# A four-layer graph network on one core: the chain of group bounds run from both ends, the whole-sum rows dealt anew, group matrices six ahead

## The chip, the cores and the metric

The kernel runs on one core of one Trainium2 chip. The metric is the device time of one execution in microseconds (us); less is better. Five engines work side by side, each in the order of its own queue: TensorE (PE in the profile), VectorE (DVE), ScalarE (ACT), GpSimd (POOL) and SyncE (SP), which issues most DMAs. An engine that comes to an instruction whose input isn't there waits, and what is queued behind waits too.

## What is computed

`x` is 2708 nodes x 128 features, `adj` a 2708 x 2708 matrix of weights at or above zero. Four layers follow each other, each `x = layernorm(x + layer(x, adj))`:

- layer 0: `D^-1/2 (adj + I) D^-1/2 x W^T + b`, with D the row sums;
- layer 1, the attention: `XW = x W`, `den[i, j] = exp(leaky_relu(s_row[i] + s_col[j]))`, `num = adj @ den`, `att = den / num`, result `adj @ (att @ XW)`;
- layer 2: a hyperbolic layer around `adj @ xt`;
- layer 3: `adj @ edge + (adj > 0) @ node + (adj < 0) @ node'` and biases.

Only the start of layer 1 is touched by the change. `exp(leaky_relu(a + b))` is the larger of `exp(a + b)` and `exp(0.01 (a + b))`, and which one it is depends on the sign of `a + b` alone. The kernel sorts the rows by one score and the columns by the other, cuts both into at most 26 matching groups of at most 126 nodes, and computes `num` for all columns group by group. For one group it needs the sum over all rows of adj weighted by exp(score), which it carries from group to group, and the group's own rows of adj.

## The kernel before

Nodes are held in NT = 22 tiles of 128 (I call one tile of rows k0 to k21) and NB = 6 column blocks of 512, the last of 148 (c0 to c5). adj is streamed from HBM in tiles `(d, c)`: block row d (4 row tiles), block column c, 1 MB each, or 0.3 MB for c5.

**After layer 0** (lines 1122 to 1162) the scores are ready. Five things then run in one stretch, from 176 to 226 us of the profile:

1. *The whole sum* (`whole_sum`, line 796, called through `sum_rows(n)`, line 1061): n row tiles are multiplied by e1 = exp(score). A row tile takes nine f32 matmuls with one output row each (line 803), dealt by `sums_of` (line 791) to the four column strips at output rows 0, 32, 64 and 96. Strips work side by side. Each strip has one block of 512 columns. Block c4 is cut by q4 = 160 into pieces of 160, 160, 160 and 32, and the last strip takes c5 (148) behind its 32. The row tiles go in the order k0-3, k16-19, k20-21, k4-7, k8-11, k12-15.
2. *The fetches* (`fetch_next`, line 764): adj doesn't fit, so block rows 0 to 3 are fetched again, in order, into 12 places of pool `keep`. A place is free once the whole sum has used up a block row (line 812). From there follow three lots. After k3: (1,2) to (1,5), (2,0), (2,1). After k19: (2,2) to (2,5), (3,0), (3,1). After k7: (3,2) to (3,5), which is 3.45 MB and the last.
3. *The group bounds* (lines 1189 to 1247). 384 sampled scores cut the sorted order. Lines 1203 to 1217 count, for each sample, how many samples lie more than CAP = 126 nodes below it (`prev`). Three PE transposes spread prev along the free axis (`prev_ps`), line 1234 copies it to `prev_row`, and a chain of GM = 26 dependent DVE steps follows: `v[g+1]` = the number of entries of prev_row below `v[g]` (line 1239). All 128 partitions do the same.
4. *The lists* (lines 1258 to 1362). From the bounds, DVE makes one-hot grids (c3, then `oh`, lines 1271 and 1277), PE makes running counts (`low`, lines 1288 and 1298), DVE turns them into slots, and for each side i = 0, 1 there are 22 pairs of a DVE one-hot tile (`ohs`, line 1326, ten buffers) and a PE matmul (`list`, line 1328). List 0 gives the row numbers for the gathers (`row_i`), list 1 the column factors `gj_l`.
5. *Spreading a score over the partitions* (lines 1226 to 1232): for each block b, PE transposes (`rb`) and an ACT Exp into `q_b`.

Who comes first on an engine is fixed by hand with `queued(engine...)` (line 190): each instruction traced inside is issued on its engine after the one that the last such block left. It is an order of issue, on engines that work in order. What isn't in such a block is placed by the framework's scheduler. The PE order before is: below, two row tiles, prev_ps, three row tiles, rb0, three, rb1, one, rb2, one, rb3, one, rb4, one, rb5, low, two row tiles, list 0 with one row tile after 8 and after 16 of its matmuls, two row tiles, list 1.

**The attention loop** (`grouped_attention`, line 1402) runs over q = 0 to 51, 26 groups for each half of the columns. Each q has an indirect gather of 128 rows of adj into `rows_g` (line 1415, three ahead), three chunks of `num` (PE 1464), a copy of two carried rows into the next group's rows_g (DVE 1467), Ln (ACT 1469), Exp of its negative (1479), a product (DVE 1483), and `uacc` (PE 1491). The first group's carried rows are copied by nine ACT copies from the whole sum (line 1371) and one DVE copy (1446). `group_matrix(dst, g)` (line 704) makes the weights of num for a group: one PE transpose (707) and one ACT Relu (708). Groups 0 to 2 are made ahead of the loop; in step q group q + 3 follows. rows_g is in pool `cb_b`, opened after `keep` is closed, on the same memory.

The rest (lines 1551 to 1887, layers 2 and 3) streams adj three times more and isn't touched.

Of the kernel before, what the change touches and what calls it, by code (L numbers as in the profile page):

```python
# [30 lines left out]
CAP = 126  # L31
FIRST = NS // P
GM = 26
SENTINEL = 1.0e29
EMPTY = -1.0e5
RC_MAX = 10.0
# [21 lines left out]
def kernel(  # L58
# [51 lines left out]
    def iota(name, n, base, step, channel, dt=F32):  # L110
        nc.gpsimd.iota(iota_i[:, :n], pattern=[[step, n]], base=base, channel_multiplier=channel)
        t = const.tile([P, n], dt, tag=name, name=name)
        nc.gpsimd.tensor_copy(t, iota_i[:, :n])
        return t

    iota_b = iota("iota_b", P, 0, 1, 0, BF16)
    part_f = iota("part_f", 1, 0, 1, 1)
    node_z = iota("node_z", NT, -N, P, 1)
    unit0 = iota("unit0", 2, 0, -1, 1)
# [577 lines left out]
    xw_i = col.tile([P, GM], I32, tag="xw_i", name="xw_i")  # L697

    flag_i = col.tile([1, 1], I32, tag="flag_i", name="flag_i")
    v = col.tile([P, GM + 1], F32, tag="v", name="v")  # L700
    sc = col.tile([P, GM], F32, tag="sc", name="sc")
    bi = col.tile([P, GM], F32, tag="bi", name="bi")

    def group_matrix(dst, g):

        pg = ps_tile(f"gb{g}")
        nc.tensor.transpose(pg[:, :P], gj_l[:, g : g + 1].to_broadcast([P, P]), ident)
        nc.scalar.activation(dst[:, g, 2:], pg[:, 2:P], AF.Relu, scale=sc[:, g : g + 1], bias=bi[:, g : g + 1])
# [75 lines left out]

    e1 = c_tile("e1")
    e2 = c_tile("e2")
    q4 = 160
    order = [0, NB - 2, NB - 1, *range(1, NB - 2)]
    steps = iter([(d, i) for d in order for i in range(len(tiles(d)))])

# [50 lines left out]
    with tc.tile_pool(name="tri", bufs=1) as tp:  # L841
# [219 lines left out]
        def sum_rows(n):  # L1061
            with queued(PE):
                return whole_sum(n)
# [104 lines left out]
    with ctx_keep:  # L1168
# [11 lines left out]
        with tc.tile_pool(name="sort", bufs=1) as st_p:  # L1180

            def srt(shape, name, dt=F32, bufs=1, tag=None):
                return st_p.tile(shape, dt, tag=tag or name, name=name, bufs=bufs)
# [7 lines left out]
            for i in range(2):  # L1191
                if i:
                    nc.tensor.matmul(below_s[i][:, :NS], lhsT=ones_b, rhs=counts[:, i, :], start=True, stop=True)
                for q in range(len(SAMPLES)):
# [5 lines left out]
                        stop=True,  # L1200
                    )

            for i in range(2):
                nc.vector.tensor_scalar(
                    lim[:, i, :], below_s[i][:, NS : NS + len(SAMPLES)], float(-CAP), None, op0=ALU.add
                )
                for q in range(len(SAMPLES)):
                    junk = srt([P, NS], f"jp{i}_{q}", F16, 2, "jk")
                    nc.vector.tensor_scalar(
                        junk,  # L1210
                        below_s[i][:, :NS],
                        lim[:, i, q : q + 1],
                        None,
                        op0=ALU.is_lt,
                        op1=ALU.add,
                        accum_out=prev[:, i, q : q + 1],
                    )
            nc.vector.tensor_tensor(prev[:, 0, :], prev[:, 0, :], prev[:, 1, :], op=ALU.max)
            prev_ps = ps_tile("prev_ps")
            sum_rows(2)  # L1220
            with queued(PE):
                for q in range(len(SAMPLES)):
                    nc.tensor.transpose(
                        prev_ps[:, q * P : (q + 1) * P], prev[:, 0, q : q + 1].to_broadcast([P, P]), ident
                    )
            for b in range(NB):
                w, cs = width(b), bslice(b)
                sum_rows(3 if b < 2 else 1)
                with queued(PE):
                    pr = bcast_block(rcl[:, 0, :], b, f"rb{b}")  # L1230
                with queued(ACT):
                    nc.scalar.activation(q_b[:, cs], pr[:, :w], AF.Exp, scale=0.99)
            prev_row = srt([P, NS], "prev_row", F16)
            nc.vector.tensor_copy(prev_row, prev_ps[:, :NS])

            nc.vector.memset(v[:, 0:1], 1.0)
            for g in range(GM):
                junk = srt([P, NS], f"jk{g}", F16, 2, "jk")
                nc.vector.tensor_scalar(
                    junk,  # L1240
                    prev_row,
                    v[:, g : g + 1],
                    None,
                    op0=ALU.is_lt,
                    op1=ALU.add,
                    accum_out=v[:, g + 1 : g + 2],
                )
# [9 lines left out]

            upto = srt([P, 2, NT], "upto")
            nc.vector.tensor_sub(upto, counted[:, :, :NT], counted[:, :, 1:])
            vs = srt([P, GM + 1], "vs")  # L1260
            nc.vector.tensor_scalar(vs, v, float(-NS), None, op0=ALU.add)
            c3 = [srt([P, NT, GM + 1], f"c3_{i}", BF16) for i in range(2)]
            val = [srt([P, NT, 6, GM], f"val{i}", BF16) for i in range(2)]
            oh = [val[i][:, :, 5, :] for i in range(2)]
# [18 lines left out]
            for i in range(2):  # L1283
                for h, (ta, tb) in enumerate(((0, t_a), (t_a, NT))):
                    low[i, h] = acc_tile(2 + 2 * i + h, f"low{i}_{ta}")
                    nn = (tb - ta) * GM
                    with queued(PE):
                        nc.tensor.matmul(
                            low[i, h][:, :nn],
                            lhsT=upper,  # L1290
                            rhs=oh[i][:, ta:tb, :],
                            start=True,
                            stop=False,
                            skip_group_check=True,
                        )
                        for t in range(tb - 1):
                            first = max(t + 1, ta)
                            nc.tensor.matmul(
                                low[i, h][:, (first - ta) * GM : nn],
                                lhsT=ones_b,  # L1300
                                rhs=oh[i][:, t, :].unsqueeze(1).to_broadcast([P, tb - first, GM]),
                                start=False,
                                stop=(t == tb - 2),
                                skip_group_check=True,
                            )

            lists = []
            for i in range(2):
# [9 lines left out]
                nc.vector.tensor_reduce(slot[:, i, :], pos[i], AX.X, ALU.add)  # L1318
                nc.vector.tensor_scalar(slot[:, i, :], slot[:, i, :], 2.0, None, op0=ALU.add)
                ps = ps_tile(f"list{i}")  # L1320
                sum_rows(2)
                for t in range(NT):
                    if i == 0 and t in (8, 16):
                        sum_rows(1)
                    ohs = srt([P, P], f"ohs{i}_{t}", BF16, 10, "ohs")
                    nc.vector.tensor_scalar(ohs, iota_b, slot[:, i, t : t + 1], None, op0=ALU.is_equal)
                    with queued(PE):
                        nc.tensor.matmul(
                            ps[:, : 6 * GM],
                            lhsT=ohs,  # L1330
                            rhs=val[i][:, t, :, :].rearrange("p n g -> p (n g)"),
                            start=(t == 0),
                            stop=(t == NT - 1),
                        )
# [53 lines left out]
    def added_up():  # L1388
        below0, okb = (c_tile(n, 1) for n in ("below0", "okb"))
        nc.vector.tensor_reduce(below0, neg_sum, AX.X, ALU.add)  # L1390
        nc.vector.tensor_scalar(below0, below0, 0.0, None, op0=ALU.is_le)
        nc.vector.tensor_scalar(okb, v[:, GM : GM + 1], float(NS), None, op0=ALU.is_equal)
        nc.vector.tensor_mul(okb, okb, below0)
        nc.vector.tensor_scalar(good, good, okb, None, op0=ALU.mult)
        nc.vector.tensor_reduce(gs, good, AX.X, ALU.add)
# [6 lines left out]
    def grouped_attention(u_sb, rows_g):  # L1402
        adj_h = adjT.rearrange("k (h w) -> (k h) w", h=2)
        chunks = [(0, BW), (BW, 2 * BW), (2 * BW, HALF)]
        with tc.tile_pool(name="main", bufs=1) as mp:
# [79 lines left out]
            def aggregate(q):  # L1485
# [12 lines left out]
                if g == GM - 1:  # L1498
                    for c, (ca, cb) in enumerate(chunks):
# [4 lines left out]
                        else:  # L1504
                            with queued(DVE):
                                nc.vector.tensor_copy(dst, src)

            for q in range(3):
                behind = gather(q)
            for g in range(3):  # L1510
# [7 lines left out]
            for q in range(2 * GM + 2):  # L1518
                if q + 3 < 2 * GM:
                    behind = gather(q + 3)  # L1520
                    if q == 3:
                        marks["begun"] = behind
                    if q + 3 < GM:
                        with queued(PE, ACT):
                            group_matrix(w_all, q + 3)
                        group_xw(q + 3, behind)
                t = q - GM - 3
                if 0 <= t < HALF // P:
                    with queued(PE, ACT):
# [444 lines left out]
```

## Time and profile before

| what | us |
|---|---|
| median of three runs (899.6, 901.1, 905.04) | 901.1 |
| the profiled execution's own time | 904.86 |
| its span, first to last instruction | 903.1 |
| PE / DVE / ACT / POOL busy in the span | 846.5 / 555.2 / 388.6 / 206.1 |
| first step of the chain of 26 begins / grid op after it begins | 184.32 / 201.61 |
| last row tile of the whole sum ends | 219.80 |
| first num matmul of the attention loop begins | 226.57 |

In a timeline a line gives the start, the time, the engine, the line of the kernel, the operation, output<-input, the shape and the number of instructions merged, and in square brackets how long the engine stood idle before it and what ended that. In the chain of waits a line gives the start, the time and the work that everything after it waited for. In the windows the columns are the busy time of PE, weight loads, DVE, ACT and POOL, then the granted share of PE's full clock (PEclk), the busy share of the DMA engines, and GB/s. An f32 matmul shows as two instructions, so a row tile has 18.

### The profile page before, as it was taken

The numbers are of one execution on the slowest core, as the hardware profiler recorded it, in microseconds if no ns is written. First come the engines' busy times: TensorE is split into PE (matmuls) and PEld (weight loads), VectorE is DVE, ScalarE is ACT, GpSimd is POOL, SyncE is SP. The second block draws the span as 40 slices with busy tenths as digits, with TensorE's granted clock in tenths as the row PEclk, the third lists the DMA queues.
The fourth block names the chain that finished last, engine by engine and source line by source line (L and its number), as shares of the span: only waits on it lengthen the run. The fifth ranks groups of instructions, "written<-read, shape, count | busy, mean of one in ns | idle before, by whom it ended". The sixth has DMA issues, their size and how long they took to land.

```text
span 903.1 us, 9464 instructions
## 1 busy us (share of the span) xinstructions
PE 846.5 (94%) x3268; PEld 430.0 (48%) x3268; DVE 555.2 (61%) x1189; ACT 388.6 (43%) x681; POOL 206.1 (23%) x176
## 2 busy tenths in 40 slices
PE   3699999698899999999999999989999899999996
PEld 3254454335344445444454444534444555555555
DVE  4777548988788888889971226375644564233313
ACT  3776433215787777777761115273332221000000
POOL 5221000101888885776500000000000000000000
PEclk9799999889899999999999999999999999999997
DMA  9995684596596555445534776496764565463410
GB/s 341 366 356 209 120 248 141 180 383 217 185 380 202 161 150 160 141 154 154 154 121 167 267 269 229 133 336 239 264 224 131 208 215 198 144 253 142 162 39 19
DMA packets 95979, 184.30 MB, mean 204 GB/s; under 512 B 6446, under 2 KB 23551, under 8 KB 95668
## 3 DMA queue, kind: packets, MB, share of 16 engines
q1 hardware_dynamic: 85700, 143.82, 46.2%
q0 software_dynamic: 8352, 37.76, 13.0%
q10 hardware_dynamic: 1872, 2.04, 0.7%
q8 instruction: 28, 0.46, 0.2%
q14 instruction: 27, 0.22, 0.1%
HBM read 179.33 MB, written 4.28 MB: 203 GB/s over the span
## 4 chain that ended last, share of the span: by engine, by line
PE 84%; DMA 9%; DVE 4%; ACT 2%; issue 0%; SPq 0%; DVEq 0%; ACTq 0%
PE a L1584 22%; PE num L1464 13%; PE uacc L1491 13%; PE a L1863 12%; PE a L866 9%; PE a L1872 6%; DMA A<-in_adjT_dram 4%; DMA B<-in_adjT_dram 3%; PE t L803 1%; DMA cb<-in_adjT_dram 1%; PE pp L1821 1%; DVE counts L1051 1%; PE mx L1691 1%; DMA rows_g<-in_adjT_dram,row_i 1%; PE su L251 0%
## 5 line engine op out<-in xcount | busy, mean ns | idle before, releaser
L1415 POOL DMA_INDIRECT rows_g<-in_adjT_dram,row_i x52 | 130.8, 2515 | 90.2 <-PE num L1464 41.2
L1469 ACT ACTIVATE ln<-num,inval,occ_l 128x512 f32<-128x512 f32 x156 | 107.4, 724 | 53.4 <-DVE rows_g L1467 49.4
L1863 PE MATMUL a<-cb,ut 128*128 128x512 f32 (+2 forms) x264 | 125.8, 559 | 1.1 <-DMA cb<-in_adjT_dram 1.1
L1491 PE MATMUL uacc<-att,xw_g 128*128 128x512 f32 (+1 forms) x312 | 126.3, 542 | 0.0
L1872 PE MATMUL a<-mask,node 128*128 128x512 f32 (+2 forms) x264 | 120.3, 537 | 0.7 <-DVE mask L1851 0.7
L1464 PE MATMUL num<-rows_g,w_all 128*128 128x512 f32 (+1 forms) x276 | 113.8, 545 | 0.8 <-ACT ln L1469 0.8
L1584 PE MATMUL a<-cb,q_b 128*128 128x512 f32 (+2 forms) x264 | 111.6, 561 | 1.8 <-DMA cb<-in_adjT_dram 1.8
L866 PE MATMUL a<-A,q_b 128*128 128x512 f32 (+2 forms) x264 | 105.9, 549 | 1.6 <-DMA A<-in_adjT_dram 1.6
L1584 PE MATMUL a<-cb,xw 128*128 128x512 f32 (+2 forms) x264 | 107.3, 550 | 0.0
L1467 DVE COPY rows_g<-num 2x512 f32<-2x512 f32 x150 | 88.0, 612 | 15.4 <-PE num L1464 14.1
L1491 PEld LDWEIGHTS uacc<-att,xw_g 128*128 128x128 f32 x312 | 59.1, 190 | 59.0 <-issue 50.0
L1483 DVE TENSOR_TENSOR att<-att,ln 128x1354 f32<-128x1354 f32 x52 | 80.5, 1548 | 2.0 <-ACT ln L1479 2.0
L1464 PEld LDWEIGHTS num<-rows_g,w_all 128*128 128x128 f32 x276 | 49.5, 190 | 54.0 <-issue 38.9
L1872 PEld LDWEIGHTS a<-mask,node 128*128 128x128 f32 (+1 forms) x264 | 48.5, 193 | 49.4 <-issue 47.6
L230 ACT ACTIVATE sq_l<-s 128x512 f32<-128x512 f32 (+1 forms) x11 | 6.6, 604 | 148.2 <-DVE s L1881 116.7
L1479 ACT ACTIVATE ln<-ln 128x1354 f32<-128x1354 f32 x52 | 69.3, 1333 | 1.7
L1851 DVE TENSOR_SCALAR mask<-cb 128x3072 fp32r<-128x3072 f32 (+5 forms) x24 | 33.5, 1395 | 59.1 <-PE a L1872 58.6
L866 PEld LDWEIGHTS a<-A,q_b 128*128 128x128 f32 (+1 forms) x264 | 45.8, 190 | 49.8 <-issue 46.4
L1584 PEld LDWEIGHTS a<-cb,q_b 128*128 128x128 f32 (+1 forms) x264 | 45.1, 192 | 46.9 <-issue 42.8
L1584 PEld LDWEIGHTS a<-cb,xw 128*128 128x128 f32 (+1 forms) x264 | 45.1, 190 | 46.5 <-issue 46.5
L1074 ACT ACTIVATE xw<-A 128x2048 f32<-128x2048 f32 (+3 forms) x36 | 57.0, 1582 | 7.9 <-DMA b_s<-in_b_dram 4.3
L1456 DVE TENSOR_SCALAR att<-q_b,gj_l 128x1354 f32<-128x1354 f32 x52 | 48.2, 927 | 12.7 <-PE uacc L1491 12.6
(445 smaller groups left out, 900.6 us busy)
## 6 DMA issues: line engine op xcount, KB each, us to landing
cb<-in_adjT_dram SPq DMA_DIRECT2D x15, 2816.0 KB
cb<-in_adjT_dram SPq DMA_DIRECT2D x15, 2560.0 KB
A<-in_adjT_dram SPq DMA_DIRECT2D x25, 1024.0 KB
B<-in_adjT_dram SPq DMA_DIRECT2D x18, 1024.0 KB
cb<-in_adjT_dram SPq DMA_DIRECT2D x3, 814.0 KB
cb<-in_adjT_dram SPq DMA_DIRECT2D x3, 740.0 KB
ut<-in_adjT_dram SPq DMA_DIRECT2D x2, 1024.0 KB
A<-in_adjT_dram SPq DMA_DIRECT2D x5, 296.0 KB
```

The lines of the kernel that those rows point to most:

```text
L866: nc.tensor.matmul(acc[c][:, :w], lhsT=z[:kw, k, :], rhs=t[:kw, i, :w], start=c not in begun, stop=(d == NB - 1 and k == NT - 1), skip_gro ...
L1074: checks[d, c] = nc.scalar.activation(below[:, :nt, :w], t[:, :nt, :w], AF.Relu, scale=-1.0, accum_out=neg_sum[:, NB * c + d : NB * c + d ...
L1415: got = nc.gpsimd.indirect_dma_start(out=gat[q], out_offset=None, in_=adj_h, in_offset=bass.IndirectOffsetOnAxis(ap=row_i[:, h, g : g + 1] ...
L1464: nc.tensor.matmul(num[:, : cb - ca], lhsT=w, rhs=gat[q][:, ca:cb], start=True, stop=True)
L1467: nc.vector.tensor_copy(gat[q + 1][0:2, ca:cb], num[0:2, : cb - ca])
L1469: nc.scalar.activation(ln_n[q][:, ca:cb], num[:, : cb - ca], AF.Ln, scale=occ_l[:, g : g + 1], bias=inval[:, g : g + 1],)
L1479: nc.scalar.activation(ln_n[q], ln_n[q], AF.Exp, scale=-1.0)
L1483: nc.vector.tensor_mul(att[q], att[q], ln_n[q])
L1491: nc.tensor.matmul(uacc[h][c][:, : cb - ca], lhsT=xw_g[:, g, :], rhs=att[q][:, ca:cb], start=(g == 0), stop=(g == GM - 1),)
L1584: nc.tensor.matmul(acc[:, :w], lhsT=weights[:kw, k, :], rhs=pc[:kw, t, :w], start=(k == 0), stop=(k == NT - 1),)
L1863: nc.tensor.matmul(acc[:, :w], lhsT=edge[:ke, k, :], rhs=pc[:ke, t, :w], start=(k == 0), stop=False, skip_group_check=True,)
L1872: nc.tensor.matmul(acc[:, :w], lhsT=node[:kw, k, j, :], rhs=mask[:kw, t - ma, :w], start=False, stop=(k == NT - 1 and j == 1), skip_group_ ...
```

## The change

- **Bounds from both ends.** `far[i, q]`, the 0/1 rows that were thrown away, are kept in BF16 (three buffers) and six ones-matmuls add them up over the partitions: `next_ps` says for each sample how many lie too far beyond it. Partitions 0 to 63 of prev_row hold prev as before, partitions 64 to 127 hold next: an ACT copy of one next_ps to SBUF and a DVE maximum with the other. The chain has GH = 13 steps, one half of the partitions going up, the other down. Two small matmuls with the constant `ends` take row 0 and row 64 of v to all partitions (`both`), and two DVE operations put the 27 bounds together. A third, `reach`, replaces the test of the last bound (line 1392).
- **Whole-sum rows.** q4 becomes 165, so that every strip has 512 + 165 columns. The PE order becomes: below, then one row tile after the first and after the second far matmul, the other far matmuls, prev_ps, three row tiles, rb0, two, rb1, both, one row tile, rb2, rb3, low, rb4, rb5, two, list 0 with one after 8 and after 16, four, list 1 with one after 8 and after 16. The order of the row tiles and the rule of the fetches stay.
- **Buffers.** ohs has four buffers instead of ten.
- **Group matrices.** Groups 3 to 5 are made ahead of the first gather, and step q makes group q + 6.

```diff
@@ the bounds @@
+            far, next_ps = {}, [acc_tile(2, "next0"), acc_tile(5, "next1")]
             for i in range(2):
...
                 for q in range(len(SAMPLES)):
-                    junk = srt([P, NS], f"jp{i}_{q}", F16, 2, "jk")
+                    far[i, q] = srt([P, NS], f"jp{i}_{q}", BF16, 3, "jp")
                     nc.vector.tensor_scalar(
...
+                    with queued(PE):
+                        nc.tensor.matmul(
+                            next_ps[i][:, :NS],
+                            lhsT=ones_b,
+                            rhs=far[i, q],
+                            start=(q == 0),
+                            stop=(q == len(SAMPLES) - 1),
+                        )
+                    if i == 0 and q < 2:
+                        sum_rows(1)
...
-            sum_rows(2)
...
-            for b in range(NB):
+            def spread_rows(b):
                 w, cs = width(b), bslice(b)
-                sum_rows(3 if b < 2 else 1)
                 with queued(PE):
                     pr = bcast_block(rcl[:, 0, :], b, f"rb{b}")
                 with queued(ACT):
                     nc.scalar.activation(q_b[:, cs], pr[:, :w], AF.Exp, scale=0.99)
+            for b in range(2):
+                sum_rows(3 - b)
+                spread_rows(b)
             prev_row = srt([P, NS], "prev_row", F16)
-            nc.vector.tensor_copy(prev_row, prev_ps[:, :NS])
+            next_row = srt([P, NS], "next_row", F16)
+            with queued(ACT):
+                nc.scalar.copy(next_row[64:, :], next_ps[0][64:, :NS])
+            with queued(DVE):
+                nc.vector.tensor_tensor(prev_row[64:, :], next_row[64:, :], next_ps[1][64:, :NS], op=ALU.max)
+            with queued(DVE):
+                nc.vector.tensor_copy(prev_row[:64, :], prev_ps[:64, :NS])
             nc.vector.memset(v[:, 0:1], 1.0)
-            for g in range(GM):
+            for g in range(GH):
...
+            both = ps_tile("both")
+            for i in range(2):
+                with queued(PE):
+                    nc.tensor.matmul(
+                        both[:, i * (GH + 1) : (i + 1) * (GH + 1)],
+                        lhsT=ends[:, i : i + 1].to_broadcast([P, P]),
+                        rhs=v,
+                        start=True,
+                        stop=True,
+                    )
+            sum_rows(1)
+            for b in range(2, NB - 2):
+                spread_rows(b)
             vs = srt([P, GM + 1], "vs")
-            nc.vector.tensor_scalar(vs, v, float(-NS), None, op0=ALU.add)
+            with queued(DVE):
+                nc.vector.tensor_scalar(vs[:, : GH + 1], both[:, : GH + 1], float(-NS), None, op0=ALU.add)
+            with queued(DVE):
+                nc.vector.tensor_scalar(
+                    vs[:, GH + 1 :],
+                    both[:, 2 * GH : GH : -1],
+                    1.0,
+                    vs[:, GH : GH + 1],
+                    op0=ALU.add,
+                    op1=ALU.max,
+                )
...
+            for b in range(NB - 2, NB):
+                spread_rows(b)
+            nc.vector.tensor_tensor(reach, vs[:, GH : GH + 1], both[:, 2 * GH + 1 : 2 * GH + 2], op=ALU.subtract)
@@ the lists @@
-                sum_rows(2)
+                sum_rows(4 if i else 2)
                 for t in range(NT):
-                    if i == 0 and t in (8, 16):
+                    if t in (8, 16):
                         sum_rows(1)
-                    ohs = srt([P, P], f"ohs{i}_{t}", BF16, 10, "ohs")
+                    ohs = srt([P, P], f"ohs{i}_{t}", BF16, 4, "ohs")
@@ the attention loop @@
+            with queued(PE, ACT):
+                for g in range(FIRST, FIRST + 3):
+                    group_matrix(w_all, g)
             for q in range(3):
                 behind = gather(q)
...
                     if q + 3 < GM:
+                        group_xw(q + 3, behind)
+                    if q + FIRST + 3 < GM:
                         with queued(PE, ACT):
-                            group_matrix(w_all, q + 3)
-                        group_xw(q + 3, behind)
+                            group_matrix(w_all, q + FIRST + 3)
```

More of the change, by code (lines that the diff above doesn't have):

```diff
@@ L33 @@
 GM = 26
+GH = GM // 2
 SENTINEL = 1.0e29
@@ L116 @@
     iota_b = iota("iota_b", P, 0, 1, 0, BF16)
+    ends = const.tile([P, 2], F32, tag="ends", name="ends")
+    nc.gpsimd.memset(ends, 0.0)
+    nc.gpsimd.memset(ends[0:1, 0:1], 1.0)
+    nc.gpsimd.memset(ends[64:65, 1:2], -1.0)
     part_f = iota("part_f", 1, 0, 1, 1)
@@ L699 @@
     flag_i = col.tile([1, 1], I32, tag="flag_i", name="flag_i")
-    v = col.tile([P, GM + 1], F32, tag="v", name="v")
+    v = col.tile([P, GH + 1], F32, tag="v", name="v")
+    reach = col.tile([P, 1], F32, tag="reach", name="reach")
     sc = col.tile([P, GM], F32, tag="sc", name="sc")
@@ L786 @@
     e2 = c_tile("e2")
-    q4 = 160
+    q4 = (N - 4 * BW) // 4
     order = [0, NB - 2, NB - 1, *range(1, NB - 2)]
@@ L1207 @@
                 for q in range(len(SAMPLES)):
-                    junk = srt([P, NS], f"jp{i}_{q}", F16, 2, "jk")
+                    far[i, q] = srt([P, NS], f"jp{i}_{q}", BF16, 3, "jp")
                     nc.vector.tensor_scalar(
-                        junk,
+                        far[i, q],
                         below_s[i][:, :NS],
@@ L1232 @@
                     nc.scalar.activation(q_b[:, cs], pr[:, :w], AF.Exp, scale=0.99)
+            for b in range(2):
+                sum_rows(3 - b)
+                spread_rows(b)
             prev_row = srt([P, NS], "prev_row", F16)
-            nc.vector.tensor_copy(prev_row, prev_ps[:, :NS])
+            next_row = srt([P, NS], "next_row", F16)
[5 more added lines that the diff above has]
+                nc.vector.tensor_copy(prev_row[:64, :], prev_ps[:64, :NS])
             nc.vector.memset(v[:, 0:1], 1.0)
-            for g in range(GM):
-                junk = srt([P, NS], f"jk{g}", F16, 2, "jk")
+            for g in range(GH):
+                junk = srt([P, NS], f"jk{g}", F16, 1, "jk")
                 nc.vector.tensor_scalar(
@@ L1391, in added_up @@
         nc.vector.tensor_scalar(below0, below0, 0.0, None, op0=ALU.is_le)
-        nc.vector.tensor_scalar(okb, v[:, GM : GM + 1], float(NS), None, op0=ALU.is_equal)
+        nc.vector.tensor_scalar(okb, reach, 1.0, None, op0=ALU.is_ge)
         nc.vector.tensor_mul(okb, okb, below0)
```

## Prediction

> **What bounds the kernel now.** I read the page first: PE is 84% of the chain that ended last, DMA 9%, and the span's second fifth is where DMA enters. The change lies there, so I read the chain of waits for 186 to 246 us, then the timelines of DVE, ACT and SP, and the windows.
>
> The timeline of DVE shows the chain of 26:
>
> ```profile
> 183.73 0.56 DVE L1234 CAST prev_row<-prev_ps 128x384 f16<-128x384 f32 x1 [1.48 <-PE prev_ps L1223]
> 184.32 0.61 DVE L1239 TENSOR_SCALAR_CACHE_REDUCE jk<-prev_row,v 128x384 f16<-128x384 f16 x1
> ...
> 200.74 0.61 DVE L1239 TENSOR_SCALAR_CACHE_REDUCE jk<-prev_row,v 128x384 f16<-128x384 f16 x1
> ...
> 201.61 0.78 DVE L1271 TENSOR_TENSOR c<-vs,upto 128x594 bf16<-128x594 f32 x1
> ```
>
> A step takes (200.74 - 184.32) / 25 = 0.657 us, 26 take 17.1. But in the chain of waits not one of them appears:
>
> ```profile
> 187.65 12.43 DMA B<-in_adjT_dram
> ...
> 202.19 12.26 DMA B<-in_adjT_dram
> 214.44 0.04 issue
> 214.49 0.41 PE t L803 x2
> 214.90 0.66 PE list L1328 x8
> 215.56 1.28 PE t L803 x15
> 216.83 0.52 PE list L1328 x6
> 217.35 2.45 PE t L803 x30
> 219.80 0.30 PE list L1328 x3
> 220.10 5.41 DMA rows_g<-in_adjT_dram,row_i
> 225.51 0.03 issue
> ...
> 225.61 0.92 DVE rows_g L1446
> ...
> 226.57 3.79 PE num L1464 x4
> ```
>
> The path is the fetches, then row tiles of the whole sum (L803), then the first gather. DVE has row_i at 218.7, yet the gather starts at 220.10, when the last row tile is done: rows_g lies on keep's memory, which the whole sum reads. So num starts 6.77 us after the last row tile, whatever the lists do. The last lot of fetches is issued when row tile k7 ends; the SP queue shows it:
>
> ```profile
> 195.50 1.18 SPq L824 DMA_DIRECT2D B<-in_adjT_dram  x1
> ```
>
> It queues behind transfers that run without a gap (about 386 GB/s from 184 to 210), so its last tile lands at 214.45. And ACT makes q_b only as PE gets to the transposes:
>
> ```profile
> 187.93 0.60 ACT L1232 ACTIVATE q_b<-rb 128x512 f32<-128x512 f32 x1 [12.28 <-PE rb L238]
> 192.23 0.60 ACT L1232 ACTIVATE q_b<-rb 128x512 f32<-128x512 f32 x1 [3.71 <-PE rb L238]
> ```
>
> The windows show PE's clock at half after idle stretches (here 197.5 to 200):
>
> ```profile
> 200.00:202.00 2.00, 1.88 (x10) 0.91 (x14) 1.86 (x8) 0.14 (x1) 0.00 (x0) 0.50 1.05 386
> 202.00:204.00 2.00, 2.00 (x20) 0.56 (x13) 1.97 (x4) 0.46 (x1) 0.00 (x0) 0.69 1.06 389
> ```
>
> [...] 0.50 at 176 to 182, 200 to 202, 224 to 230. [...] In the trace ACT stands 12.28 us in front of the first Exp; nothing overtakes. [...] here x_d is issued at 169.20 and bytes move from 170.0, 0.8 us, which I use.
>
> **The change, part by part.**
>
> *Where the chain starts.* The ACT copy of next_row is queued(ACT) behind the Exp of rb0 and of rb1. Those wait for PE: rb1 stands behind five row tiles. So the chain no longer waits for prev_ps alone but for all of that. PE: far matmuls and the first two row tiles at half clock, as now (4.42 us for two), plus six far matmuls (0.2 to 0.3 each) and a wait for the third far buffer, end with prev_ps at 185.1 (now 183.7). Three row tiles 3.6 (now 183.62 to 187.24) give 188.7, rb0 0.6, two row tiles 2.45, and rb1 starts at 191.7. Exp starts 0.7 later (as 191.54 to 192.23), takes 0.6: 192.95. The copy, by the nearest ACT rows (256 columns 0.38, 512 columns 0.60), 0.5: 193.4. DVE maximum and cast of 384 columns, 0.56 each as L1234: chain start 194.5, against 184.3. **+10.2.**
>
> *The chain.* 13 x 0.657 = 8.5 instead of 17.1: **-8.55.** It ends at 203.05 instead of 201.35.
>
> *Both and vs.* Two f32 matmuls with 14 columns on a cold PE, unpriced in the trace: between 0.3 (a warm transpose) and 0.9; I take 0.6. One more DVE operation, 0.1 to 0.2. Grids start at 204.1 instead of 201.6: **+2.5** in all.
>
> *Up to low.* PE has stood idle since 192.3, over 10 us, so it is at half clock. Behind `both` stand a row tile (2.2 cold, half of 4.42), rb2 and rb3 (0.6 each, rb3 perhaps one Exp later for its buffer): low starts at 207.5, now 204.0. It takes 5.9 as now, and ends at 213.4 instead of 209.9. [...]
>
> *The last lot of fetches.* Now k7 ends before low. In the new order k6 and k7 come after low, rb4 and rb5: 213.4 + 0.85 + 2 x 1.24 = 216.7, against 195.5. The transfers before it have run dry by about 205.5 (214.45 less 3.45 MB at 386 GB/s, 8.9 us). So its bytes lie bare: 216.7 + 0.8 + 8.9 + 0.8 for the end (bytes thin out by 213.7, landing 214.45) = 227.2, against 214.45.
>
> *What PE has after low.* Ten row tiles instead of six, and both lists in front of the end. k6, k7, list 0 with k8, k9, then k10 and k11 end at 224.2; k12 needs the fetch. From its landing: rest of k12 0.4, k13 to k15 3.6, 16 list matmuls. Four ohs buffers let PE run only four ahead of DVE (0.17 each), so 8 take about 0.97 instead of 0.66. Sum 5.95, and I add 0.6 for a clock that may drop again while PE waits (0 to 1.8). The last row tile ends at 233.8, now 219.80: **+14.0.** Were the fetch in time, PE alone would end it at 231.0, +11.2.
>
> *The gather and the start of the loop.* 6.77 as now. Beside it run list 1's end, gj_l, the nine ACT copies (3.6) and now seven group matrices instead of four, three more of 0.44 on ACT: 3.6 + 0.35 + 7 x 0.42 = 6.9 on ACT, about equal to the gather's cover. **+0.2** (0 to 1.4).
>
> *Group matrices.* Their place in a step is unchanged, so the wait of num for the ACT Relu (2.12 us at 234) stays. Steps 20 to 22 lose theirs; a step takes about 4.71 with one (4.66, each fifth 4.93) and 4.55 without: 3 x 0.16, **-0.5.** *q4:* 677 columns instead of 692, 2% of a row tile, already in the sums. reach, ends and the other test: a few 0.1 us operations on DVE and POOL, both with idle time near them; uncovered they would cost under 0.5.
>
> Sum: 14.0 + 0.2 - 0.5 = **+13.7**. On the profile's own 904.86 (span 903.1, 1.8 around it) that is 918.6; the profiled run lies 3.8 above the median of the runs, so on the median **914.8**. About 1% is what a measurement of this kernel can tell from no change.
>
> **Rivals.**
>
> 1. *The copy isn't held* (chance 0.13): it gets in front of the Exps, because ACT is idle from 175.6 to 187.9. For: its input is ready at 184. Against: the queued block. Then the chain runs 185.9 to 194.4, grids at 195.5, low ends at 203.6, the fetch is issued at 206.9, lands at 217.4, and the last row tile ends at 223.4: +3.6 + 0.2 - 0.5, **904.4**. Even so no gain.
> 2. *The saving reaches the path* (0.05): grids at 195.5 instead of 201.6, -6.1, with -0.5 from the group matrices: **894.5**. It decides if k7 ends before 205.5, when the transfers run dry, and the last row tile before 213.7. For: DVE is over 90% busy in that stretch. Against: the chain of waits has no L1239, and after low stand ten row tiles.
> 3. *The queue holds but the fetch is hidden* (0.2, part of the likeliest): PE alone, +11.2 + 0.2 - 0.5, **912**.
>
> **How the numbers follow.** The copy held with the fetch bare has 0.60, with the fetch hidden 0.20; together 910.5 to 919.5, from the clock (-0.6 to +3.2), both (±0.3) and the loop's start (up to 1.2). Rival 1 has 0.13, rival 2 0.05, 0.02 is left for more. Slower by over 1% (above 910.1): 0.74. Within 1%: rival 1, most of rival 2 and the low end of the likeliest, 0.22. Faster: 0.04. The range reaches down to rival 1: 904 to 919.5.
>
> **What would show it.** Right: ACT's next_row copy right behind the second q_b Exp near 193; 13 steps from about 194; PE idle between rb1 and both; a hole in the DMA share from about 206 to 217; the last row tile near 234. Wrong: next_row before q_b; the last lot issued before 206; a gather that starts ahead of the last row tile.

## The result and the profile after

The kernel after takes 916.76 us (median of four runs, 914.91 to 921.35), the kernel before 903.07 us (four runs, 899.6 to 905.37). The ratio is 1.0151, with a 95% interval of 1.0123 to 1.0178: the change makes the kernel slower by about 1.5%. The prediction's 914.8 was reckoned from a median of 901.1 for the kernel before.

The profiled execution after took 921.35 us (span 919.6). It is the highest of the four, 4.6 above their median, so its places are read here against the profiled execution of before (904.86), a difference of 16.5 us. The table gives each place from the start of the first `below` matmul, which is at 177.73 us before and at 178.33 after.

| us from the first `below` | before | after | later by | predicted |
|---|---|---|---|---|
| chain begins | 6.59 | 18.04 | 11.45 | 10.2 |
| grids begin | 23.88 | 28.20 | 4.32 | 2.5 |
| low ends | 32.23 | 38.24 | 6.01 | 3.5 |
| last row tile ends | 42.07 | 59.03 | 16.96 | 14.0 |
| num begins | 48.84 | 65.82 | 16.98 | 14.2 |

From the first num to the last uacc it is 247.38 before and 248.19 after (+0.8), from there to the end 429.15 and 427.26 (-1.9). With the 0.6 by which the stretch begins later, 16.98 + 0.6 + 0.8 - 1.9 = 16.5, the whole difference. That last part of the kernel isn't touched; in the profiles of all kernels here it lies between 424.9 and 429.2, so it varies by 4 us of itself.

The timeline of ACT after answers the two q_b lines of before. The copy stands right behind the second Exp, as its queue has it, and the third Exp waits until 209:

```profile
190.95 0.60 ACT L1248 ACTIVATE q_b<-rb 128x512 f32<-128x512 f32 x1 [14.70 <-PE rb L244]
194.07 0.60 ACT L1248 ACTIVATE q_b<-rb 128x512 f32<-128x512 f32 x1 [2.52 <-PE rb L244]
194.69 0.47 ACT L1258 CAST next_row<-next 64x384 f16<-64x384 f32 x1
209.47 0.60 ACT L1248 ACTIVATE q_b<-rb 128x512 f32<-128x512 f32 x1 [14.30 <-PE rb L244]
```

By the page, DVE's share of the chain of waits has gone from 4% to 7%. The chain of waits after has the steps of the chain of bounds (L1266) in it, which it lacked before. From there it goes through `both`, low, two row tiles (k6 and k7) and the bare fetch to the end of the lists:

```profile
193.45 0.59 PE rb L244 x4
...
196.37 0.63 DVE jk L1266 x2
...
205.01 1.00 PE both L1291 x4
...
217.28 2.43 PE t L810 x30
...
220.41 11.08 DMA B<-in_adjT_dram
...
237.70 5.45 DMA rows_g<-in_adjT_dram,row_i
```

The SP queue issues the first tile of the last lot as k7 ends, 23.9 us later than before (195.50):

```profile
219.39 0.37 SPq L831 DMA_DIRECT2D B<-in_adjT_dram  x1
```

The windows after (PE, weight loads, DVE, ACT, POOL, PEclk, DMA share, GB/s) show what lies on both sides of it:

```profile
196.00:205.00 9.00, 0.00 (x0) 0.02 (x1) 8.40 (x27) 0.00 (x0) 0.00 (x0) 0.59 1.06 378
...
211.00:213.00 2.00, 2.00 (x25) 1.45 (x24) 1.25 (x3) 2.00 (x15) 0.00 (x0) 0.95 0.00 0
...
206.00:220.00 14.00, 14.00 (x155) 8.51 (x154) 10.97 (x26) 8.18 (x50) 0.00 (x0) 0.81 0.02 5
```

While the chain runs, PE does nothing. After it, PE works at half clock until about 211.2 (0.50 from 205 to 211, 0.95 as the mean of 211 to 213). For 14 us the DMA engines carry 5 GB/s; in the ten us after that, the last lot, 316.

What PE waited for in this stretch stands in its own timeline, in the square brackets:

```profile
205.01 1.00 PE L1291 MATMUL both<-v,ends 128*128 128x14 f32 x4 [10.98 <-DVE jk L1266]
...
231.53 0.79 PE L810 MATMUL t<-B,e 128*1 128x165 f32 x20 [1.71 <-DMA B<-in_adjT_dram]
```

So PE stood 10.98 us for the chain, but only 1.71 for the fetch: most of the hole in the transfers lies under PE's own late work. One window each, from the first `below` to the last row tile, first before, then after:

```profile
177.73:219.80 42.07, 39.66 (x462) 18.12 (x463) 37.86 (x136) 10.18 (x55) 1.80 (x1) 0.90 0.88 322
178.33:237.37 59.04, 44.50 (x488) 20.95 (x489) 32.89 (x123) 10.37 (x56) 1.81 (x1) 0.84 0.64 227
```

Of the 17 us that the last row tile came later, PE was idle for 12.1 (14.54 instead of 2.41) and busy for 4.8 more.

### The profile page after: what moved, and what is told of

Its sections match the earlier page's. It is cut to its first block, busy times and chain, and to the rows that moved or that the text cites. A ratio compares the mean times of both kernels' runs of the same rounds, so it can differ in the third digit from the quotient of the medians.

```text
span 919.6 us, 9493 instructions
## 1 busy us (share of the span) xinstructions
PE 849.2 (92%) x3278; PEld 429.4 (47%) x3278; DVE 548.1 (60%) x1166; ACT 389.3 (42%) x682; POOL 206.3 (22%) x179
## 3 DMA queue, kind: packets, MB, share of 16 engines
q0 software_dynamic: 8352, 37.76, 12.8%
## 4 chain that ended last, share of the span: by engine, by line
PE 84%; DVE 7%; DMA 6%; ACT 2%; issue 1%; DVEq 0%; ACTq 0%
PE a L1643 22%; PE num L1519 13%; PE uacc L1546 13%; PE a L1922 11%; PE a L873 9%; PE a L1931 6%; DMA A<-in_adjT_dram 4%; PE t L810 2%; DMA B<-in_adjT_dram 1%; PE pp L1880 1%; DVE counts L1058 1%; DVE jk L1266 1%; PE mx L1750 1%; PE su L257 1%; PE low L1349 1%; DMA rows_g<-in_adjT_dram,row_i 1%
## 5 line engine op out<-in xcount | busy, mean ns | idle before, releaser
L1470 POOL DMA_INDIRECT rows_g<-in_adjT_dram,row_i x52 | 133.7, 2571 | 106.6 <-PE list L1383 57.6
```

What stands on the lines that cost most here:

```text
L1470: got = nc.gpsimd.indirect_dma_start(out=gat[q], out_offset=None, in_=adj_h, in_offset=bass.IndirectOffsetOnAxis(ap=row_i[:, h, g : g + 1] ...
```

## The experiments

The theory after the result: two things in the new queue orders cost the time. The ACT copy stands behind two Exps and holds the chain (the hold), and the row tiles k6 and k7, which free the memory for the last lot, stand behind low (the rows). The rivals: it is the slower lists with four ohs buffers, the group matrices, or a shorter chain that pays as soon as it is let go. Unless said otherwise, "before" is the kernel before in runs on the same chip. All these kernels compute the whole result.

### The hold taken away

In the kernel after, the copy is put on ACT's queue ahead of the first Exp:

```diff
+            next_row = srt([P, NS], "next_row", F16)
+            with queued(ACT):
+                nc.scalar.copy(next_row[64:, :], next_ps[0][64:, :NS])
             for b in range(2):
                 sum_rows(3 - b)
...
-            next_row = srt([P, NS], "next_row", F16)
-            with queued(ACT):
-                nc.scalar.copy(next_row[64:, :], next_ps[0][64:, :NS])
```

> The changed kernel with one move: the ACT copy of next_row is traced ahead of rb0 and rb1, so that it is queued in front of both Exps. Theory (the copy is held behind the Exps): it runs near 185.5 on the changed kernel's clock, the 13 steps begin near 187.6 instead of 196.4, the grids near 197.6 instead of 206.5, the last lot of fetches goes out near 210 instead of 219.4, lands near 222, and the last row tile ends near 228 instead of 237.4: about 9 us less than the changed kernel, 907 to 908, still 3 to 5 us above before, since k6 and k7 stay behind low. Rival (the hold doesn't matter, the row tiles behind low alone cost the time): within 3 us of the changed kernel.

Measured: 910.8 us against 903.75, 1.0068 (1.0042 to 1.0095). About half of the loss is gone. The time is some 3 us above the 907 to 908 that were expected; the last row tile ends at 227.0 in the trace, near the 228 expected. The chain begins 9.11 us after the first `below` (18.04 after). The last row tile ends at 49.47 instead of 59.03, still 7.4 later than before. The SP queue of this kernel shows when the last lot is issued:

```profile
208.38 0.37 SPq L831 DMA_DIRECT2D B<-in_adjT_dram  x1
```

And its windows show the hole in the transfers (DMA share 0.17):

```profile
206.00:210.00 4.00, 3.86 (x51) 1.67 (x53) 2.88 (x15) 1.38 (x9) 0.00 (x0) 1.00 0.17 13
```

The chain now ends at 195.2, 6 us sooner than before (201.4), and yet the last lot is issued 13 us later, since k6 and k7 still stand behind low; the hole in the transfers is about 5 us long instead of 14 (an estimate: at the share of 1.05 that the transfers have in the windows of before, 0.17 as the mean of 206 to 210 and 0.87 as that of 196 to 206 put it from 204.3 to 209.4).

### The rows put back, the hold kept

In the kernel after, the three row tiles k5 to k7 come ahead of `both`:

```diff
+            sum_rows(3)
             both = ps_tile("both")
...
-            sum_rows(1)
             for b in range(2, NB - 2):
                 spread_rows(b)
...
-                sum_rows(4 if i else 2)
+                if i:
+                    sum_rows(4)
```

> The changed kernel with one move: row tiles k5, k6 and k7 stand in front of both, in the stretch in which PE is idle, instead of behind both and behind low. The copy stays held. Theory (a late k7 lays the last lot of fetches bare): the last lot goes out near 198, the DMA share has no hole, it lands near 215; the chain of 13 still begins near 196.4; low begins near 208 and the last row tile ends near 231 instead of 237.4, about 6 us less than the changed kernel, near 911. Rival (the fetch is not on the path, the chain's late start is all): the last row tile moves by less than 3 us.

Measured: 914.63 us against 903.75, 1.0112 (1.0089 to 1.0134); near 911 had been expected. The last row tile ends 4.4 us sooner than after, where 6 were expected. The last lot goes out 20.9 us sooner (its second tile at 198.99, after at 219.86), and no fetch stands in its chain of waits. But PE is idle again from about 198 until `both` at 205.6, and the first `low` products take nearly twice as long. I put that down to a clock at half (an estimate from the times alone). In this chain of waits 18 take 3.47 us, in that of the kernel without the hold 1.91:

```profile
209.06 3.47 PE low L1349 x18
```

The 4.4 us aren't the fetch alone. The three row tiles also fill time in which PE had stood idle, as its timeline shows (10.98 us in the kernel after):

```profile
205.60 1.00 PE L1292 MATMUL both<-v,ends 128*128 128x14 f32 x4 [7.39 <-DVE jk L1266]
```

The wait for `both` is 3.6 us shorter, the one for the fetch (1.71) is gone, and other things, the slow `low` products above all, take back 0.9. By these waits the larger part of what the rows cost is PE's own work that came too late, the smaller part the transfers.

### Both

> Both moves: the copy ahead of the Exps, and k5 to k7 in front of both. Theory: the two causes are all of the loss up to a rest that stems from ten row tiles' worth of PE work and from list 1 standing in front of the last row tile. Chain from 187.6, grids near 199, low ends near 207, fetch landed near 215, last row tile near 223.5 against 219.8 before (clocks differ by 0.6): 14 us less than the changed kernel, 903 to 905. Rival (a chain of 13 pays once it is freed): below 899.

The edit is the two diffs above together. Measured: 904.52 us against 903.75, 1.0006 (0.9985 to 1.0026). The last row tile ends at 45.38, 13.65 sooner than after; the two moves alone brought 9.56 and 4.44, together 14.0. So at the last row tile the two add up, and they are 13.65 of the 16.96 us. In the medians the two moves alone brought 6.6 and 2.8 of the 13.7 us and together 12.9; the intervals are too wide to say more. The other 3.31 us at the last row tile don't show in the time: the last part of the kernel, which isn't touched, took 424.9 in this profile and 429.15 before. k14 and k15 behind list 1 and the four ohs buffers cost 3.35 and 1.27 in experiments of their own below, which is more than enough for it. No fetch is left in the chain of waits in front of the gather; in this stretch of the windows the transfers have a share of 1.05, as in the windows of before, and PE's clock is at 1.00 (from 200 to 204 they are 1.07 and 1.00):

```profile
204.00:208.00 4.00, 3.55 (x47) 2.84 (x46) 4.00 (x12) 3.96 (x27) 0.00 (x0) 1.00 1.05 385
```

It also answers the rival of the shorter chain. Here the chain ends at 18.24, 5.4 us sooner than before (23.62), and `low` at 28.02, 4.2 sooner, and nothing of that reaches the last row tile or the time. `both` itself starts 1.4 us after the chain's end, since it stands behind the row tile k7.

### The hold alone, in the kernel before

The kernel before keeps its 26 steps on all partitions. Only the copy of prev_row goes from DVE to ACT, behind the second Exp:

```diff
+                if b == 2:
+                    with queued(ACT):
+                        nc.scalar.copy(prev_row, prev_ps[:, :NS])
...
-            nc.vector.tensor_copy(prev_row, prev_ps[:, :NS])
```

> The kernel before with 26 steps and its own order of row tiles, but with prev_row copied by ACT, queued behind the Exp of rb1, instead of by DVE. Theory (the chain's start is worth its full delay once the slack in front of low, about 1.1 us, is gone): the chain begins near 193.4 instead of 184.3, low ends near 219 to 220 instead of 210, with PE's clock at half in its first part, the last lot of fetches goes out as before (near 195.5) and lands in time, and the last row tile ends 8 to 10 us later: near 912. Rival (the chain is covered, as it is not in the chain of waits of before): less than 3 us.

Measured: 914.07 us against 904.89, 1.0086 (1.0064 to 1.0108). The chain begins 9.4 us later; low begins 8.3 later, so the chain had 1.1 us to spare, and low takes 8.6 instead of 5.95. Its first 18 products with `ones_b` take 3.91 us in the PE timeline and the next 21 1.49, where before has 2.07 and 0.88; the rest go as fast as before. That is nearly twice the time, so I put it down to a clock at half (an estimate from these times). The last row tile and num are each 10.4 late. One line of ACT order costs this without any other part of the change. The 26 steps now stand in the chain of waits:

```profile
194.56 0.48 ACT prev_row L1231
195.07 0.63 DVE jk L1241 x2
```

### The row tiles ahead of list 1

Does the first gather hang on the last row tile, as I took it to? In the kernel after, all six last row tiles come ahead of list 1:

```diff
-                sum_rows(4 if i else 2)
+                sum_rows(6 if i else 2)
                 for t in range(NT):
-                    if t in (8, 16):
+                    if i == 0 and t in (8, 16):
```

> The changed kernel with one move: k14 and k15 stand in front of list 1 with the other four row tiles, instead of behind its 8th and 16th matmul. Theory (the first gather waits for the last row tile, not for the lists): the last row tile ends near 235.3 instead of 237.4, the gather starts 0.3 later, and num starts about 2 us earlier although list 1 ends about 0.6 later; time 1.5 to 2 us below the changed kernel. Rival (list 1 and the group matrices set num's start): num starts up to 0.6 us later.

Measured: 918.28 us against 903.75, 1.0153 (1.0124 to 1.0182), the same as after, where 1.5 to 2 us less had been expected. The tie is real: the last row tile ends 3.35 us sooner and the gather begins 3.39 sooner. But num begins only 1.4 sooner. Now list 1 ends last, and its factors gj_l open the group matrices, which stand ahead of num in this chain of waits:

```profile
238.44 0.42 PE list L1383 x2
...
240.16 0.23 ACT gj_l L1414
...
243.93 3.43 PE num L1519 x4
```

The expected gain went into a new wait, on matrices of which the change had just put three more ahead of the loop.

### The small parts

Group matrices six ahead, in the kernel before (the hunk of the change, three more ahead of the loop and step q making group q + 6):

> The kernel before with the group matrices six ahead and nothing else. Theory: three steps of the loop lose their matrix (0.16 each), and three more are made while the first gather is under way; num starts 0 to 0.6 later, the loop is 0.5 to 0.9 shorter, the time is 0 to 0.9 us below before. Rival (six ahead takes the wait of num for the ACT Relu out of the loop's start): the 2.1 us wait at the second num goes, and the time falls by 2 us or more.

Measured: 902.25 us against 904.89, 0.9977 (0.9956 to 0.9998). The loop is 1.0 shorter (246.37), its start 1.0 later (49.86), so the stretch as a whole gains nothing. What the profile is shorter by, 2.2 us, lies ahead of the first `below` (at 175.59, before at 177.73), where nothing was changed; the 2.6 us between the medians aren't shown to come from the matrices. The wait of num for the Relu is still there, as this line of its PE timeline shows (predicted: it stays):

```profile
232.61 1.68 PE L1464 MATMUL num<-rows_g,samples 128*128 128x512 f32 x4 [2.28 <-ACT w_all L708]
```

The even deal on top of it:

```diff
-    q4 = 160
+    q4 = (N - 4 * BW) // 4
```

> As the run before, and q4 = 165 as well, again on the kernel before. Theory: 15 of 692 columns fewer in each row tile, 0.026 us each; only the four or five row tiles after the last fetch lie on the path, 0.1 us, so no difference to the run before that can be measured. Rival (all 18 row tiles are on the path): another 0.5 us.

Measured: 903.95 us against 904.89, 0.9985 (0.9974 to 0.9996); no difference to the one before it can be told. The last row tile ends at 42.17, before at 42.07.

Four ohs buffers instead of ten, in the kernel before:

```diff
-                    ohs = srt([P, P], f"ohs{i}_{t}", BF16, 10, "ohs")
+                    ohs = srt([P, P], f"ohs{i}_{t}", BF16, 4, "ohs")
```

> The kernel before with four ohs buffers instead of ten, and nothing else. Theory: a batch of 8 list matmuls takes 1.25 us instead of 0.66 and one of 6 takes 0.9 instead of 0.5; list 0's last 14 stand between the last landing and the last row tile, so that ends about 1 us later and num starts 1 us later: 0.1%, hardly to be measured in the time, plain in the trace. Rival: DVE sets the pace of the lists anyway and nothing moves.

Measured: 904.32 us against 904.65, 0.9997 (0.9985 to 1.0008). The trace does show it. In this kernel's PE timeline eight list matmuls take 1.32 us where the same line of before has 0.72; the last row tile is 1.27 later, num 1.68. In the time it can't be found. The line of before comes first:

```profile
212.35 0.72 PE L1328 MATMUL list<-val,ohs 128*128 128x156 bf16 x8
...
212.18 1.32 PE L1328 MATMUL list<-val,ohs 128*128 128x156 bf16 x8
```

### What is left of the idea

First, both moves, the row tiles ahead of list 1, and eight ohs buffers (their room comes from letting `jp` and `jk` share three buffers):

```diff
-                    far[i, q] = srt([P, NS], f"jp{i}_{q}", BF16, 3, "jp")
+                    far[i, q] = srt([P, NS], f"jp{i}_{q}", BF16, 3, "jk")
...
-                junk = srt([P, NS], f"jk{g}", F16, 1, "jk")
+                junk = srt([P, NS], f"jk{g}", BF16, 3, "jk")
...
-                    sum_rows(4)
+                    sum_rows(6)
...
-                    if t in (8, 16):
+                    if i == 0 and t in (8, 16):
...
-                    ohs = srt([P, P], f"ohs{i}_{t}", BF16, 4, "ohs")
+                    ohs = srt([P, P], f"ohs{i}_{t}", BF16, 8, "ohs")
```

> The changed kernel with both moves (copy ahead of the Exps, k5 to k7 in front of both), k14 and k15 ahead of list 1, and eight ohs buffers (the far rows share the buffers of the chain's thrown-away output). Theory: the lists cost PE about 1.2 us less ahead of the last row tile and 2.5 us of list 1 go behind it; the last row tile ends about 41.5 us after the first below matmul against 42.1 before, num starts within 0.5 us of before, and the time is that of before within 1 us. Rival (the short chain pays at last): 2 us or more below before.

Measured: 902.78 us against 904.89, 0.9981 (0.997 to 0.9992). The last row tile ends at 40.62, 1.45 sooner than before, num begins at 48.57, 0.27 sooner. The median is 2.1 us below before, where at most 1 had been expected; that is the number of the rival (2 us or more), but not its reason, since num's start hardly moves. In the profile 1.0 of the 2.1 lies ahead of the first `below` (176.69) and 0.5 in the loop. In its chain of waits the seven matrices stand in front of num, not the gather:

```profile
221.95 0.23 ACT gj_l L1415
...
225.00 0.47 PE gb L714
225.47 4.53 PE num L1520 x6
```

Then the same with the matrices three ahead again, as before:

```diff
-            with queued(PE, ACT):
-                for g in range(FIRST, FIRST + 3):
-                    group_matrix(w_all, g)
...
                     if q + 3 < GM:
+                        with queued(PE, ACT):
+                            group_matrix(w_all, q + 3)
                         group_xw(q + 3, behind)
-                    if q + FIRST + 3 < GM:
-                        with queued(PE, ACT):
-                            group_matrix(w_all, q + FIRST + 3)
```

> The run with both moves, packed lists and eight ohs buffers, but with the group matrices three ahead as before. In that run num's start hung on seven group matrices behind gj_l, no longer on the gather. Theory: with four of them num starts 1 to 1.5 us earlier, the loop is 0.5 to 0.9 longer: 0 to 1 us below that run, about 2.5 us below the kernel before. Rival (the gather or the carried rows become the limit at once): num starts less than 0.5 us earlier, and the time is 0.5 us above that run.

Measured: 900.33 us against 904.65, 0.9963 (0.9946 to 0.9981). It is the fastest version here, ahead of both kernels, if by little; its interval overlaps those of the version before it and of the matrices six ahead alone, so it isn't shown to be faster than these. num begins at 47.29, 1.55 sooner than before. The gain in time is put at 1.7 to 4.9 us by the interval (0.0019 and 0.0054 of 904.65), and 1.55 is just below that. In the profile, the fastest of this version's runs, the rest lies in parts that these edits hardly touch: 2.9 us ahead of the first `below` (174.82), which lies between 174.8 and 179.3 in the twelve profiles, and 2.0 after the last uacc. How much of the 1.55 is the shorter chain's isn't shown, since no run has this order with 26 steps; `both` stands behind k7 here too, until 1.4 us after the chain's end.

## Why the prediction was right

The direction, the mechanism and the size held. The medians differ by 13.7 us, the predicted sum. The sum was made for the profiled execution, though, and there it is 16.5; the sizes below were mostly too small, and that the medians agree to the tenth is partly luck: the profiled execution of after lies 4.6 above its median, that of before 1.8. By its steps:

- **Where the chain starts.** Right in kind: the copy waits behind the Exps, shown by the ACT timeline, by taking the hold away (-8.9 at the chain's start) and by making it alone (+9.4). It came 1.25 later than predicted. Of this 1.0 is there when prev_ps ends (186.74, 8.41 after the first `below`; 7.4 predicted): one wait for a `far` buffer was reckoned with, and DVE waited twice for one that PE still read. The DVE timeline after has 1.47 and 1.32 us:

```profile
183.13 0.62 DVE L1217 TENSOR_SCALAR_CACHE_REDUCE jp<-below,lim 128x384 bf16<-128x384 f32 x1 [1.47 <-PE next L1227]
185.09 0.62 DVE L1217 TENSOR_SCALAR_CACHE_REDUCE jp<-below,lim 128x384 bf16<-128x384 f32 x1 [1.32 <-PE next L1227]
```

- **The chain.** -8.55 predicted, -8.54 measured.
- **Both and vs.** Mis-sized: 1.00 us for `both` instead of 0.6 (its bound was 0.9), and with vs and the waits between, the grids came 4.32 later than before instead of 2.5. 1.25 of the 1.8 came from the chain's start.
- **Up to low.** Mis-sized: low ends 6.0 later, not 3.5. Of the 2.5 between them 1.8 are those of the grids. The other 0.7 fit the clock: it came back only at about 211.2, 6.2 us after `both` began, so rb2 and rb3 took 1.90 us instead of 1.2 and low's first products ran at half clock (0.50 from 205 to 211). Low had been reckoned at 5.9 as before, where the clock is 1.00 from 204 to 210. The range given for the clock (-0.6 to +3.2) was an estimate.
- **The last lot of fetches.** Right: issued at 219.39 where 216.7 was predicted, with the hole from 206 to 220. But its price was smaller than the hole looks: PE waited 1.71 us for it, where 2.8 were reckoned (14.0 less 11.2). From issue to the last landing it took 12.1 us, not 10.5: the bytes moved until about 229.3 and the last tile landed at 231.49.
- **What PE has after low.** Mis-sized: from the end of low to the last row tile it took 20.8 us, without the wait for the fetch 19.1, where 17.6 were reckoned (213.4 to 231.0). Eight list matmuls took 1.32 us instead of 0.97, four times over, which is nearly all of it.
- **After the landing.** Last row tile 5.87 later; 5.95 predicted, plus 0.6, an estimate, for a clock that did not drop (1.00 from 229 to 238).
- **The gather and the start of the loop.** 6.78, as 6.77. That it hangs on the last row tile is shown by putting the tiles ahead of list 1; that the seven matrices were just covered, by what happened then.
- **Group matrices.** -0.5 predicted. In the eight profiles with matrices six ahead the loop takes 246.85 us in the mean (246.37 to 248.19, the highest being after), in the four with three ahead 247.55 (247.07 to 248.68): -0.7, with a scatter of its own size.

*The rivals.* The second, that the saving reaches the path, is refuted: with hold and rows both gone the chain ends 5.4 sooner and the ratio is 1.0006. The first, the copy not held, is what the first experiment made. Its mechanism was right, but not its price, 904.4: measured were 910.8, and the last row tile came 7.4 late where I had 3.6. I had k7 at 206.9 and the fetch landing at 217.4; it was 208.4 and 221.2, so from issue to landing it took 12.8 us instead of 10.5; from the landing to the last row tile it was 5.8, as reckoned (6.0). The third, the fetch hidden, missed by the 1.71 us for which PE waited. Its size was off too: without this wait the last row tile would still have ended about 15.3 later (an estimate, 16.96 less 1.71), not 11.2.

What stays open is why the profiled execution lies 4.6 us above the median of its runs. Ten ohs buffers in the changed kernel weren't tried, nor was the order of the last version with a chain of 26 steps, which would tell what the shorter chain is worth there.

## What to carry to other kernels

Look first whether the work that you shorten is in the chain of waits; halving 17 us of hidden steps was worth nothing here even with the two orders put right (1.0006). When an order of issue is written by hand, ask of every instruction put into it what the one ahead of it waits for, since a half-microsecond copy behind an Exp inherited ten. And ask of every piece of work that is moved back what it sets free: two row tiles moved behind low laid bare the last 3.45 MB of transfers. Then look in the engine's own timeline for what it really waited: the hole in the transfers was 14 us long, PE's wait for them 1.71, and the 11 us in which PE had no row tile queued ahead of `both` cost more.

## What the runs showed of the hardware that I had not expected

- PE's clock took 6.2 us of work to come back after an idle stretch of 11 us (205.0 to 211.2, windows after). PE had been idle since 194.03. The clock was still 1.00 from 196 to 197, then 0.78 from 197 to 198, 0.50 from 198 to 211, 0.89 from 211 to 212 and 1.00 from 212 to 213. From these means I put the fall at 197.6 and the return at 211.2, so it was at half for 13.6 us, 6.2 of them with PE at work.
- The prediction takes the half clock of before at 200 to 202 for the result of an idle stretch from 197.5 to 200. The PE timeline of before doesn't show one. The longest idle stretch there is 1.70 us, followed by 0.45 of work and another 0.51:

```profile
199.16 0.45 PE L803 MATMUL t<-B,e 128*1 128x160 f32 x8 [1.70 <-DMA B<-in_adjT_dram]
```

PE was busy for 1.91 of the 4 us from 196 to 200, and the clock fell all the same (0.98 over these 4 us, 0.50 over the next 2). What made it fall isn't shown.

- Two f32 matmuls with only 14 columns took 1.00 us in the kernel after, where the clock was 0.50 (205 to 206). In the chains of waits of the first and third experiment they took 0.59 and 0.56; PE had been idle for 2.30 us before them in the first, and in the third it came straight from row tiles.
- A producer that feeds PE through four buffers instead of ten makes eight list matmuls take nearly twice as long (1.32 against 0.72, PE timelines of the two kernels): behind a row tile PE then waits for DVE to fill a buffer, 0.27 us in the chain of waits after.
